# Two feature products made early, the count products moved behind x1's, and another start value for a planner's DMA clock

## The chip, the cores and the metric

One Trainium2 chip, of which one core runs the program. The metric is the time on the device in microseconds (us), the median over runs; less is better.

## The reference

A graph with 4096 nodes and 64 features, and a dense 4096 x 4096 matrix `adj` whose entries are mostly zero. Two layers, cut to what matters:

```python
# layer 0: two hops
h = relu(layernorm(x)); u = h
for k in range(2):
    u = tanh(concat([adj @ u, u], axis=1) @ W[k])     # x1, then x2
x = x + u
# layer 1
h = relu(layernorm(x)); support = h @ weight
mask = (adj != 0)
rank = cumsum(mask, axis=1); deg = rank[:, -1:]
k = minimum(deg, 100.0)
pos = rank - (deg - k)
w = mask * where(pos > 0, 0.5 ** (k - pos), 0.0)
x = x + w @ support + bias
```

## The kernel before, in words

The nodes are cut into four rows (`NCH`) of 1024 and 32 blocks (`NB`) of 128. A tile of the matrix holds one block of sources by 1024 destinations, 512 KB, and the loads of the first sweep take two blocks at once, 1 MB. Every load is issued on SyncE's queue (SP).

**Sweep 1** goes through the four rows, 16 pairs of blocks each (step `k` counts 64 pairs). For each pair TensorE (PE) adds `adj @ h` into the row's sums. A row's sums are `acc = (acc[0], acc[1])`: `acc[1]` is one PSUM bank where the two halves of 512 destinations (`c` = 0, 1) stand in partitions 0 to 63 and 64 to 127 (64-column products, L264); `acc[0]` has two banks for the blocks whose x1 is already known, where h and x1 are multiplied in one go (128-column products, L473, the "fused" blocks). Beside it VectorE (DVE) and ScalarE (ACT) mark the nonzero entries as bytes and DVE counts along them (`count_pair`), which yields codes that layer 1 turns into weights. In row 0 further work is strung between the pairs by `k`: layer norms, `features_T` (h transposed into `pre1`), and `own_share`, which multiplies a row's transposed features with the second half of W[0] and puts the product back into `pre1`.

**The end of a row** is the generator `finish_row`; sweep 1 takes one step of it per pair (`step()`), so that its parts lie between the next row's pairs. `x1_of` multiplies the sums into the bank `po`, takes in the own product, and makes tanh: rows 1 and 2 have their own product from `own_share` and DVE adds it (L221), rows 0 and 3 make it as a second product in `po` (L210). `totals` adds up the counts. `x1_and_share` makes x1 as nodes and its share of hop 2 (banks `pt`, L327), `take` copies them out on ACT. At the end `set_after` multiplies the totals with a triangle matrix (banks `pb`, L303: how many nonzeros stand in partitions behind) and makes the row's limits on DVE (L305 to L316). `settle` (L402) subtracts these limits from the codes.

**Sweep 2** starts with row 3's end (`finish_last`, the same parts in one generator, stepped after blocks 1, 3 and 5), then has two kinds of work for PE: 72 single blocks for hop 2 (`hop`, L264, each with its own load of 512 KB, L817) and 128 units of layer 1 (`layer1`, L739, 128 columns wide, each with a weight tile made by ACT, L679, or DVE, L671 and L674). When a row's hop 2 is complete, `finish_x2` makes x2, the residual, the second layer norm and the features of layer 1 (`feat`, L612 and L613).

The order of all this in sweep 2 is written out by a planner that runs when the program is built: `clock` holds a rough time for each engine and for the DMA queue, `use` advances it, and at each step the planner takes the next block if its tile should have landed (`tiles[n][3]`) or the next unit if its weights and features should be ready. The engines then run their instructions strictly in that order, whatever the real times are. Lines that matter for it:

```python
        clock["DMA"] = -7.0
...
            end = use("DMA", 1.28, t)
            tiles.append((k, r, a, end + (2.0 if t > start else LAND)))
...
            if n in (1, 3, 5):
                next(last, None)
```

Zero of these clocks is the first block of sweep 2. The last 56 units of layer 1 are kept for after the last block (`n_late`).

PSUM has two single banks, `one` and `two`, that all small products share, beside two buffers each of `acc[0]` and `acc[1]`.

Of the kernel before, what the change touches and what calls it, by code (L numbers as in the profile page):

```python
# [44 lines left out]
def gnn_kernel(  # L45
# [20 lines left out]
    nc = tc.nc  # L66
# [66 lines left out]
    def two(name="two"):  # L133
        return pone.tile([P, C], F32, tag="two", name=name)
# [68 lines left out]

    by_t = lambda ap: ap.rearrange("q (u p v) -> q u v p", u=2, v=2)

    def paired(po, terms):

        for n, (w, v) in enumerate(terms):
            for c in range(NC):
                nc.tensor.matmul(  # L210
                    po[c * D : (c + 1) * D, :], w(c), v(c),
                    start=n == 0, stop=n == len(terms) - 1,
                )

    def x1_of(po, I, terms, xs, at_=None):


        own = (lambda c: wz[:, c, 0, 1], lambda c: flat(pre1[:, chunk(I), :]))
        paired(po, terms + [own] * (at_ is None))
        if at_ is not None:  # L220
            nc.vector.tensor_tensor(at_, po, flat(pre1[:, chunk(I), :]), op=ALU.add)  # L221
            po = at_
        for c in range(NC):
            nc.scalar.activation(xs[c][:D], po[c * D : (c + 1) * D, :], AF.Tanh)

    def own_share(I):

        h = flat(pre1[:, chunk(I), :])
        po = two(name="po")
        paired(po, [(lambda c: wz[:, c, 0, 1], lambda c: h)])  # L230
        nc.scalar.copy(h, po)

    as_nodes = lambda ap: ap.rearrange("p (c t) e -> p t c e", c=NC)

# [61 lines left out]
        nc.vector.tensor_tensor(both.bitcast(U16), count(I, 0), count(I, 1), op=ALU.add)  # L296
        nc.scalar.copy(tot, both)

    def set_after(I, tot, banks):

        cols = slice(I * CW, (I + 1) * CW)
        for c, pb in enumerate(banks):
            nc.tensor.matmul(pb, tri, tot[:, c * C : (c + 1) * C], start=True, stop=True)  # L303
        for c, pb in enumerate(banks):
            nc.vector.tensor_scalar(  # L305
                after[1][:, cols][:, c * C : (c + 1) * C], pb, off, float(K), op0=ALU.add, op1=ALU.min
            )

        early = after[0][:, cols]
        nc.vector.tensor_scalar(  # L310
            early.bitcast(U16), count(I, 1), -1.0, float(FULL * 257), op0=ALU.mult, op1=ALU.add
        )
        nc.vector.tensor_tensor(
            early.bitcast(U16), early.bitcast(U16), after[1][:, cols].bitcast(U16), op=ALU.add
        )
        nc.vector.tensor_scalar(early, early, float(K), None, op0=ALU.min)  # L316
# [24 lines left out]
    def finish_row(I, acc, held):  # L341
        if I:

            T = [tmp(name="T") for _ in range(NC)]
            for c in range(NC):
                nc.scalar.copy(T[c][:D], acc[0][:D, c, :])
                nc.scalar.copy(T[c][D:], acc[1][c * D : (c + 1) * D])
            xs = [tmp(name="x1T") for _ in range(NC)]
            for c in range(NC):
                nc.scalar.copy(xs[c][D:], acc[0][D:, c, :])  # L350
            terms = [(lambda c: w0, lambda c: T[c])]
        else:
            xs = [tmp(name="x1T") for _ in range(NC)]
            S = tmp(name="S")
            nc.scalar.copy(S, acc[1])
            terms = [(lambda c: wz[:, c, 0, 0], lambda c: S)]
        both = tmp([P, CW], U8, name="both")
        yield
        x1_of(one(name="po"), I, terms, xs, T[1] if 0 < I < NCH - 1 else None)
        tot = tmp([P, CW], BF16, name="tot")  # L360
        totals(I, both, tot)
        yield
        if I:
            yield
        banks = x1_and_share(I, xs)
        take(hxs[I][:, :, D:], banks, 0)
        if I == 0:
            yield

            own = [v for k in sorted(held) for v in held[k]]  # L370
            for n, (b, a) in enumerate(own):
                agg_pair(acc[0][:, 0, :], at(b)[:, D:], a, n == 0, n == len(own) - 1)
            held.clear()
            G = tmp(name="G")
            nc.scalar.copy(G, acc[0][:, 0, :])
            yield
            g = by_t(G)
            for h, pt in halves_of(banks, 1):
                for t in range(2):
                    nc.tensor.matmul(  # L380
                        pt[:, t], g[:, h, t, :], wz[:, :, 1, 0, :],
                        start=False, stop=True, skip_group_check=True,
                    )
        take(pre1[:, chunk(I), :], banks, 1)
        yield
        set_after(I, tot, [one(name="pb"), two(name="pb")])
        all_settle(I)


# [18 lines left out]
    def sweep1():  # L408
# [28 lines left out]
        for k, (I, b) in enumerate(pairs):  # L437
            n = k % (NB // 2)
            if n == 0:
                acc = sums_of("acc")  # L440
            if k == 0:
                load(1, 0)
                load_x(2)
                load(2, 0)
                load_x(1)
                load(3, 0)
                load_x(0)
            if k == 6:
                load_weights()
            load(k + 5, k)  # L450
            if k == 0:
                next(first)
                next(first)
                rest = ln_relu(hxs[-1][:, : CB - 2, :D], pre1[:, NB - CB : b0, :])
                next(rest)
                for _ in first:
                    pass
                next(rest)
                more = ln_relu(hxs[2][:, :, :D], pre1[:, chunk(2), :])
                for _ in rest:  # L460
                    pass
                next(more)
                steps.append(more)
            if k in (2, 5):
                q = 1 - k // 3
                steps.append(ln_relu(hxs[q][:, :, :D], pre1[:, chunk(q), :]))
            a = tiles[k]
            count_pair(I, b, a, k in marked)
            for r in (1, 0):
                g = b - 1 + r  # L470
                if fused(I, g):
                    for c in range(NC):
                        nc.tensor.matmul(  # L473
                            acc[0][:, c, :], at(g), a[:, r, c * C : (c + 1) * C],
                            start=g == CB * I - 1, stop=g == 0,
                        )
                else:
                    agg_pair(acc[1], at(g)[:, :D], a[:, r], g == NB - 1, g == CB * I)
                if I == 0 and g < CB:
                    held.setdefault(k, []).append((g, a[:, r]))  # L480
            step()
            if k in (4, 6, 9, 13):
                features_T({4: 3, 6: 2, 9: 1, 13: 0}[k])
            if k in (12, 14):
                own_share({12: 2, 14: 1}[k])

            j = k + (2 if k < NB // 2 - 2 else 3)
            if j < len(tiles):
                m = j % (NB // 2)
                if m % 2 == 1 and m >= 3 if j < NB // 2 else m % 3 == 2 and m > 3:  # L490
                    mark_on_act(*pairs[j], tiles[j])
                    marked.add(j)
            if I > 1 and n % 2 == 1:
                settle()
            if n == NB // 2 - 1 and I < NCH - 1:
                steps.append(finish_row(I, acc, held))
                step()
# [12 lines left out]
    def finish_last(acc):  # L510

        I = NCH - 1
        bytes_ = mbuf.rearrange("p a r i -> p (a r i)")
        tot = bytes_[:, 2 * CW :].bitcast(BF16)
        totals(I, bytes_[:, :CW], tot)
        T, xs = ([tmp(name=n) for _ in range(NC)] for n in ("T", "x1T"))
        for c in range(NC):
            nc.scalar.copy(T[c][:D], acc[0][:D, c, :])
            nc.scalar.copy(T[c][D:], acc[1][c * D : (c + 1) * D])
        for c in range(NC):  # L520
            nc.scalar.copy(xs[c][D:], acc[0][D:, c, :])
        use("ACT", 3.4, 0.2)
        yield
        x1_of(one(name="po"), I, [(lambda c: w0, lambda c: T[c])], xs)
        use("ACT", 1.1, use("PE", 1.8) + 0.2)
        yield
        banks = x1_and_share(I, xs)
        take(hxs[I][:, :, D:], banks, 0)
        take(pre1[:, chunk(I), :], banks, 1)
        use("ACT", 1.5, use("PE", 2.0) + 0.2)  # L530
        yield
        set_after(I, tot, [one(name="pb"), two(name="pb")])
        feats[2] = place([P, CB, 2 * D], F32R, "cnt", "feat")
        use("DVE", 2.9, use("PE", 0.5) + 0.2)
        all_settle(I)
        space(feats[2].rearrange("p b d -> p (b d)"), clock["DVE"], 2)

# [262 lines left out]
    def sweep2(acc):  # L800
# [9 lines left out]
        total = len(blocks)  # L810
        accs, tiles, open_ = {}, [], {}
        n_late = 56
        clock["DMA"] = -7.0

        def load(k, r, a, t):
            I, b = blocks[len(tiles)]
# [133 lines left out]
```

## Time and profile before

| | |
|---|---|
| median of 3 runs | 349.91 us (349.72 to 350.49) |
| the profiled execution | 349.67 us |
| its span in the profile | 347.9 us |
| PE busy | 327.6 us (94%) |
| DVE, ACT busy | 266.3 us (77%), 202.9 us (58%) |
| granted TensorE clock | 0.996 |
| HBM read | 107.15 MB |
| end of row 0's loading, first block of sweep 2, last block landed | 54, 199, 308 us |

The profile is one execution of the program. An engine's busy time is the union of its instructions; "PEld" is the loading of weights into PE, beside the products. A line of the chain of waits gives a start, a duration, an engine, the tile that is written, the source line and the number of instructions. A float32 product of 512 columns shows as two matmuls. A line of the timeline ends, in brackets, with the idle time before it and what ended that. A line of the waits gives the waiting engine and line, what it waited for, the total in us, how often, and the longest.

### The profile page before, as it was taken

The page shows a single profiled execution, that of the slowest core. Times are in us where ns is not written, and L with a number is a line of the kernel's source. Part 1 is how long each engine was busy: PE and PEld are TensorE (multiplying, and loading weights), DVE is VectorE, ACT ScalarE, POOL GpSimd, SP SyncE. Part 2 cuts the span into 40 slices and gives each one's busy share as a digit, 9 for nine tenths or more (in the row PEclk, how much of TensorE's full clock was granted, in tenths as well). Part 3 has the DMA queues.
Part 4 walks back from the last instruction along what each step waited for, and adds up shares of the span by engine and source line. Part 5 has one row for each costly group of instructions (what it writes and reads, how often), then busy time and mean ns, then how long its engine had stood idle before and what let it go on. Part 6 is the DMA issues. An engine that isn't in the chain of part 4 may idle for free.

```text
span 347.9 us, 3823 instructions
## 1 busy us (share of the span) xinstructions
PE 327.6 (94%) x1360; PEld 155.6 (45%) x1360; DVE 266.3 (77%) x392; ACT 202.9 (58%) x207; POOL 23.8 (7%) x22
## 2 busy tenths in 40 slices
PE   2787899999999999999999999989999999989995
PEld 0132334333434344444444443334466645347885
DVE  4987688549959999989999927785398998269733
ACT  2097885094437634167144253256599999799940
POOL 2220200000000000000000000403000030003000
PEclk9999999999999999999999999999999999999998
DMA  7999999999999979893998899999975448930012
GB/s 255 413 409 406 411 408 410 407 410 408 409 410 409 398 303 382 304 356 121 381 338 309 298 386 367 342 417 407 409 300 183 179 145 314 401 140 0 3 43 77
DMA packets 30466, 108.44 MB, mean 312 GB/s; under 512 B 2416, under 2 KB 3824, under 8 KB 30448
## 3 DMA queue, kind: packets, MB, share of 16 engines
q1 hardware_dynamic: 30448, 108.21, 80.5%
q8 instruction: 10, 0.16, 0.2%
q14 instruction: 8, 0.07, 0.1%
HBM read 107.15 MB, written 1.05 MB: 311 GB/s over the span
## 4 chain that ended last, share of the span: by engine, by line
PE 77%; DMA 16%; DVE 2%; ACT 1%; issue 1%; POOL 1%; SPq 1%; DVEq 0%; ACTq 0%
PE acc L473 24%; PE accl L739 17%; PE acc L264 16%; PE acc_low L264 12%; DMA codes<-in_adjA_dram 11%; DMA ring<-in_adjA_dram 5%; PE pt L327 2%; PE po L210 2%; PE pto L787 2%; PE py L566 1%; POOL s L197 1%; PE pb L303 1%; ACT codes L241 1%; DVE feat L613 0%; DVE xc L200 0%
## 5 line engine op out<-in xcount | busy, mean ns | idle before, releaser
L679 ACT ACTIVATE weights<-codes 128x1024 fp32r<-128x1024 uint8 x95 | 91.6, 1044 | 14.5 <-DVE codes L402 7.8
L473 PE MATMUL acc<-ring,hx 128*128 128x512 f32 x176 | 76.4, 594 | 0.0
L264 PE MATMUL acc<-ring,hx 128*64 128x512 f32 x288 | 66.6, 599 | 0.9 <-DMA ring<-in_adjA_dram 0.9
L739 PE MATMUL accl<-weights,feat 128*128 128x512 f32 x254 | 62.4, 398 | 0.4 <-DVE feat L613 0.4
L739 PEld LDWEIGHTS accl<-weights,feat 128*128 128x128 f32 x254 | 46.3, 188 | 18.6 <-ACT weights L679 6.1
L473 PEld LDWEIGHTS acc<-ring,hx 128*128 128x128 f32 x176 | 33.4, 190 | 42.3 <-issue 42.2
L264 PE MATMUL acc_low<-codes,hx 128*64 128x512 f32 x192 | 46.1, 597 | 4.4 <-DMA codes<-in_adjA_dram 2.6
L264 PE MATMUL acc_low<-ring,hx 128*64 128x512 f32 x128 | 34.5, 657 | 9.5 <-DVE hx L200 6.2
L402 DVE TENSOR_TENSOR codes<-codes,after 128x2048 uint16<-128x2048 uint16 x32 | 38.1, 1219 | 0.1
L264 PEld LDWEIGHTS acc<-ring,hx 128*64 128x64 f32 x288 | 19.4, 136 | 39.3 <-issue 32.2
L242 ACT ACTIVATE codes<-codes 128x2048 uint8<-128x2048 int8 x19 | 36.3, 1910 | 0.6
L250 DVE TENSOR_SCALAR mbuf<-ring 128x2048 uint8<-128x2048 f32 x30 | 36.6, 1220 | 0.0
L674 DVE TENSOR_SCALAR weights<-bits 128x1024 fp32r<-128x1024 f32 x32 | 22.2, 695 | 15.0 <-PE accl L739 11.6
L241 ACT ACTIVATE codes<-ring 128x2048 int8<-128x2048 f32 x8 | 15.3, 1911 | 30.3 <-DMA ring<-in_adjA_dram 30.3
L257 DVE TENSOR_TENSOR codes<-mbuf,cnt 128x1024 uint16<-128x1024 uint16 x41 | 28.4, 692 | 1.5
L258 DVE TENSOR_SCALAR cnt<-codes 128x1024 uint16<-128x1024 uint16 x64 | 27.3, 427 | 2.2
L264 PEld LDWEIGHTS acc_low<-codes,hx 128*64 128x64 f32 x192 | 14.2, 137 | 29.7 <-issue 19.5
L241 ACT ACTIVATE codes<-codes 128x2048 int8<-128x2048 f32 x11 | 21.0, 1913 | 9.6 <-DMA codes<-in_adjA_dram 9.6
L587 POOL TENSOR_TENSOR pre<-pre,wb 128x512 f32<-128x512 f32 x4 | 5.2, 1295 | 266.3 <-DVE xc L192 266.3
L264 PEld LDWEIGHTS acc_low<-ring,hx 128*64 128x64 f32 x128 | 9.4, 147 | 29.9 <-issue 13.5
L671 DVE TENSOR_SCALAR bits<-codes 128x1024 uint32<-128x1024 uint8 x32 | 22.1, 691 | 0.7
L250 DVE TENSOR_SCALAR mbuf<-codes 128x2048 uint8<-128x2048 f32 x15 | 18.3, 1220 | 0.0
(87 smaller groups left out, 233.6 us busy)
## 6 DMA issues: line engine op xcount, KB each, us to landing
ring<-in_adjA_dram SPq DMA_DIRECT2D x74, 512.0 KB, 6.0
ring<-in_adjA_dram SPq DMA_DIRECT2D x37, 1024.0 KB, 8.2
codes<-in_adjA_dram SPq DMA_DIRECT2D x26, 1024.0 KB, 17.4
pre<-in_x_dram SPq DMA_DIRECT2D x4, 256.0 KB, 7.3
xres<-in_x_dram SPq DMA_DIRECT2D x4, 256.0 KB, 7.3
out_dram<-o SPq DMA_DIRECT2D x3, 256.0 KB, 2.6
out_dram<-o SPq DMA_DIRECT2D x2, 128.0 KB, 2.2
wb<-in_weights_dram SPq DMA_DIRECT2D x1, 192.0 KB, 17.9
```

The source lines that it names most:

```text
L241: nc.scalar.activation(sign, a, AF.Sign)
L242: nc.scalar.activation(m, sign, AF.Square, scale=float((FLAG - 1 + 0.25) ** 0.5))
L250: nc.vector.tensor_scalar(m, a, 0.0, float(FLAG - 1), op0=ALU.not_equal, op1=ALU.mult)
L257: nc.vector.tensor_tensor(q, m, cnt, op=ALU.add)
L258: nc.vector.tensor_scalar(cnt, q, 0x7F7F, None, op0=ALU.bitwise_and)
L264: nc.tensor.matmul(acc[c * D : (c + 1) * D, :], src, a[:, c * C : (c + 1) * C], start=first, stop=last,)
L402: nc.vector.tensor_tensor(q, q, a[:, None, :].to_broadcast([P, 4, CW // 2]), op=ALU.subtract)
L473: nc.tensor.matmul(acc[0][:, c, :], at(g), a[:, r, c * C : (c + 1) * C], start=g == CB * I - 1, stop=g == 0,)
L671: nc.vector.tensor_scalar(state["bits"], q, float(ZERO), ONE, op0=ALU.subtract, op1=ALU.mult)
L674: nc.vector.tensor_scalar(w, state["bits"].bitcast(F32), 2.0 ** (127 - LOW), None, op0=ALU.mult)
L679: nc.scalar.activation(w, q, AF.Exp, scale=LN2, bias=BIAS)
L739: nc.tensor.matmul(sums[g][:, c, :], feats[J][:, k, :], w[:, c * C : (c + 1) * C], start=first, stop=last,)
```

## The change

Own products: `own_share` is now also called for row 3 (step 10) and for row 0 (step 15). Row 3's product goes back into `pre1`, as those of rows 1 and 2 do, and its x1 takes DVE's addition. Row 0's stays in the bank `one` as an unfinished sum; the product with the row's sums is added in the same bank later. Count products: the two matmuls of `set_after` become `count_after`, which stands directly behind `x1_and_share`, and write into the banks of the row's sums, which have been read by then, instead of `one` and `two`. DVE's part stays where it was. The planner's costs for these parts follow, and its clock for the DMA queue starts at −10.5 instead of −7.0.

```diff
-    def paired(po, terms):
+    def paired(po, terms, first=True, last=True):
...
-                    start=n == 0, stop=n == len(terms) - 1,
+                    start=first and n == 0, stop=last and n == len(terms) - 1,
...
     def x1_of(po, I, terms, xs, at_=None):
-        own = (lambda c: wz[:, c, 0, 1], lambda c: flat(pre1[:, chunk(I), :]))
-        paired(po, terms + [own] * (at_ is None))
+        paired(po, terms, at_ is not None)
...
+    own0 = []
+
     def own_share(I):
         h = flat(pre1[:, chunk(I), :])
-        po = two(name="po")
-        paired(po, [(lambda c: wz[:, c, 0, 1], lambda c: h)])
-        nc.scalar.copy(h, po)
+        po = two(name="po") if I else one(name="po")
+        paired(po, [(lambda c: wz[:, c, 0, 1], lambda c: h)], last=I > 0)
+        if I:
+            nc.scalar.copy(h, po)
+        else:
+            own0.append(po)
...
-    def set_after(I, tot, banks):
-
-        cols = slice(I * CW, (I + 1) * CW)
+    def count_after(I, tot, acc):
+
+        banks = [acc[0][:, c, :] for c in range(NC)] if I else [acc[1], acc[0][:, 1, :]]
         for c, pb in enumerate(banks):
             nc.tensor.matmul(pb, tri, tot[:, c * C : (c + 1) * C], start=True, stop=True)
+        return banks
+
+    def set_after(I, banks):
+
+        cols = slice(I * CW, (I + 1) * CW)
...
     # finish_row
-        x1_of(one(name="po"), I, terms, xs, T[1] if 0 < I < NCH - 1 else None)
+        x1_of(one(name="po") if I else own0.pop(), I, terms, xs, T[1] if I else None)
...
         banks = x1_and_share(I, xs)
+        counts = count_after(I, tot, acc)
...
-        set_after(I, tot, [one(name="pb"), two(name="pb")])
+        set_after(I, counts)
...
     # sweep1
-            if k in (12, 14):
-                own_share({12: 2, 14: 1}[k])
+            if k in (10, 12, 14, 15):
+                own_share({10: 3, 12: 2, 14: 1, 15: 0}[k])
...
     # finish_last
-        x1_of(one(name="po"), I, [(lambda c: w0, lambda c: T[c])], xs)
-        use("ACT", 1.1, use("PE", 1.8) + 0.2)
+        x1_of(one(name="po"), I, [(lambda c: w0, lambda c: T[c])], xs, T[1])
+        use("ACT", 1.1, use("DVE", 0.7, use("PE", 0.9) + 0.2) + 0.1)
         yield
         banks = x1_and_share(I, xs)
+        counts = count_after(I, tot, acc)
...
-        use("ACT", 1.5, use("PE", 2.0) + 0.2)
+        use("ACT", 1.5, use("PE", 2.4) + 0.2)
         yield
-        set_after(I, tot, [one(name="pb"), two(name="pb")])
+        set_after(I, counts)
         feats[2] = place([P, CB, 2 * D], F32R, "cnt", "feat")
-        use("DVE", 2.9, use("PE", 0.5) + 0.2)
+        use("DVE", 2.9, clock["PE"])
...
     # sweep2
-        clock["DMA"] = -7.0
+        clock["DMA"] = -10.5
```

## The prediction, made before the changed kernel was run

> **What bounds the kernel now.** I read the page's busy times first, then the waits of TensorE from the end of row 0's loading on, then the chain of waits, and last the timeline around the places that the change touches.
>
> ```profile
> PE 327.6 (94%) x1360; PEld 155.6 (45%) x1360; DVE 266.3 (77%) x392; ACT 202.9 (58%) x207; POOL 23.8 (7%) x22
> ```
>
> ```profile
> PE accl L739 <- DVE feat L613: 1.6, 2, 1.1
> PE acc L264 <- DMA ring<-in_adjA_dram: 0.9, 2, 0.8
> PE po L210 <- ACT S L355: 0.3, 1, 0.3
> ```
>
> The three lines are all that TensorE (PE) waited for from 54 to 345 us: 2.8 us. From row 0's finish on the kernel is a queue of PE work, and whatever leaves that queue shortens it. Before 54 us it is otherwise: PE was busy 40.2 of 54.4 us there (windows), waiting for tiles of the matrix that land about every 2.6 us. Work put there, before the last tile of row 0, can be free. The chain of waits prices what the change moves:
>
> ```profile
> 54.40 1.94 PE po L210 x8
> 56.34 1.72 PE acc_low L264 x8
> ...
> 102.23 1.23 PE po L210 x3
> ...
> 109.40 1.87 PE acc_low L264 x8
> 111.27 0.54 PE pb L303 x2
> 111.80 7.02 PE acc_low L264 x32
> ...
> 201.00 2.09 PE po L210 x7
> ```
>
> Row 0 makes two products into po (1.94); row 1 makes one (1.23, and 0.37 behind one interleaved matmul: 1.60 together); row 3 makes two (2.09 and 0.38, 2.47). A pair of blocks takes 1.72 behind other 64-column work but 1.87 behind 128-column work such as pt or pb; the eight-matmul groups in 7.02 are 4 x 1.72 and again 0.14 more. So a change of width into the narrow products costs 0.15. The two count matmuls stand between narrow pairs in every row and pay it.
>
> ```profile
> 41.26 1.91 ACT L242 ACTIVATE codes<-codes 128x2048 uint8<-128x2048 int8 x1
> ...
> 43.73 1.06 PE L210 MATMUL po<-pre,wz 128*64 128x512 f32 x4
> ...
> 44.44 1.91 ACT L241 ACTIVATE codes<-codes 128x2048 int8<-128x2048 f32 x1 [1.27 <-DMA codes<-in_adjA_dram]
> ...
> 53.29 0.57 ACT L231 COPY pre<-po 128x512 f32<-128x512 f32 x1
> ...
> 227.76 0.73 PE L739 MATMUL accl<-feat 128*128 128x512 f32 x2 [1.15 <-DVE feat L613]
> ```
>
> ACT has a hole of 1.27 us before 44.44, set by a landing. PE stands idle 1.15 us at the start of layer 1, waiting for features.
>
> **The change part by part.** The sum is made against the profiled execution: 349.67 us, a span of 347.9 and 1.8 around it. It is 0.24 under the median of the three runs, 349.91. 0.2% is 0.7 us, about what can be told from no change (the runs lie 0.8 apart).
>
> *Row 0's own product.* Its four matmuls (1.06 us busy, 0.86 of the queue's pitch: half a pair's 1.72) go from behind S to the end of row 0's last pair, about 51.5 us. There PE waits for the next tile until 52.11, and then for S until 54.40 (0.35). S itself is set by ACT (own copy of row 1 at 53.29 to 53.86, then S), which nothing here lengthens. The pair at 52.1 starts perhaps 0.3 later and still ends before 54.4. Gain 0.86; if S came earlier, the cover would be 0.3 thinner. Bank and operand are ready: features of row 0 are copied at 48.67 to 49.32.
>
> *Row 3's own product into row 0.* It is issued behind the tenth pair, near 38.5 us; the next pair waits for its landing at 39.34, so 0.1 at most is pushed. Its ACT copy (0.57, as L231) queues behind the mark that ends at 43.17 and ends at 43.74, inside the 1.27 hole; behind it on ACT is the mark at 44.44, which waits for its data anyway. Row 2's own product needs the same bank: it ran at 43.73, so it moves 0.1. Row 1's own product waited 0.6 for the copy before it (PEld po, ACT pre), which takes that up. Cost 0; without that cover, 0.57.
>
> In row 3's finish 0.87 of PE goes (2.47 to 1.60). In its place DVE adds (0.69) before tanh. Row 2, which does this already, shows po at 148.18, add at 150.05, tanh at 150.78 to 152.06: 3.88 us from po to x1. Put at row 3's po, 200.83, x1 is ready at 204.71, against 204.76 now; but the two blocks between now end at 204.3. PE would wait 0.45 before pt. Net gain 0.4. Queued behind the add on DVE are about five subtractions of L402 (1.22 each), then the row's limits: 203.4 + 6.1 = 209.5, and they start at 209.54 now. Nobody is delayed, and nobody gains.
>
> *Counts behind pt.* Both are 128 columns wide, so two width changes per row go: 0.15 into the narrow pairs and about 0.11 into pb (0.54 against two 512-column passes of 0.215). 0.25 a row, 1.0 for four rows; in row 0 the 0.65 of pb may give 0.1 more, left out. The bounds are 0 (if pt's drain is only moved) and 0.4. The operand tot is there: cast at 57.48 to 58.51 in row 0, at 105.95 to 106.99 in row 1, while pt ends at 60.1 and 109.4. The new banks were last read by copies that x1 needed. DVE idles 7.7 and 6.95 us for pb now (L305); in row 0 it would run ahead, but PE, and not DVE, sets that stretch.
>
> *New clock.* No work changes; the order of PE's queue does. Up to tile 41 the planner counts tiles as 1.28 us apart from its start value, so from −7.0 tile 23 is expected at 27.6 and tile 33 at 41.0 us after the first block, from −10.5 at 24.1 and 37.5. The trace has the first block at 199.06 and tile 23 landing at 225.12 (26.1), tile 24 at 226.37 (27.3), tile 33 at 239.87 (40.8). With row 3's 0.87 off, the loads that wait for its blocks come that much earlier: 25.2, 26.4, 39.9. So the old clock is late by up to 2.4 and the new one early by 1.1 to 2.4. What it wins: tile 24 is planned ahead of layer 1's start, so one block (0.86) fills the 1.15 hole; I take 0.5 of it, bounds 0 and 1.15. What it costs: a block queued before its tile stalls PE. The traced blocks in 28 to 49 us start 0.40 to 1.99 after landing at the ends of their bursts; shifted by 3.5 − 0.87 and a lag of PE behind the plan of 0.3 to 1.0, they would be up to 1.5 too early. Tiles land 1.28 apart, so a stall is paid once and not for each tile. I take 0.7, bounds 0 and 2.4.
>
> For tile 31 fifteen of the sixteen landing updates are in at 235.97 and the last at 237.31; it stays 1.3 behind to tile 49. One late DMA engine thus makes the 2.4.
>
> **Sum.** 0.86 + 0.4 + 1.0 + 0.5 − 0.7 = 2.1. 349.67 − 2.1 = 347.6; from the median 347.8. I say 347.6.
>
> **Rivals.** *Late tiles take about half of it.* Stall 1.5 to 2.4 instead of 0.7: 348.4 to 349.3. For it: one lagging engine, as traced. Against it: the lag is not the clock's doing and may fall elsewhere.
>
> *Slower by the new order.* The blocks moved forward outrun their tiles in the first half (2.4), and the last ten blocks do too: there the traced blocks start 0.04 to 0.6 after landing, waits 0.9 in all, the loads being released by blocks twelve and more before them. If the new order sends that release 2 us later against the blocks, each late tile is waited for: 2.4 + 2.0 against gains of 2.8, so 1.6 slower, 351.3. It decides once stalls together exceed 3.5. The last tile is followed by a fixed 56 units of layer 1, so nothing wins it back. Against it: the loads at the end are released by consumption, not by the rough clock.
>
> *Slower tiles.* If the pitch that the planner sees were not 1.28 but 1.39, as (260.92 − 210.83)/36 from tile 13 to 49 with all interruptions, and the lag of 1.3 came on top again, tile 33 would be another 20 x 0.11 = 2.2 late: stall 2.9, time 349.8. Against it: between the interruptions the landings keep 1.28, 410 GB/s. The Trainium skill, DMA: Bandwidth & Descriptors, Specifications, gives a core some 358 GB/s of HBM, an estimated 1.46 us for such a tile of 512 KB, by which the stall would be near 4 and the time 351; here the trace disagrees with it.
>
> *Nothing arrives at the end.* The last of the 72 tiles lands at 308.41 and PE waits for it. If the loads there are what counts and not PE, 349.2 to 350.6. Against it: each load there waits for a block of PE, so it moves with PE.
>
> *The parts don't act.* Pt's drain stays and x1 of row 3 is no sooner: 0.86 and 0.5 − 0.7, 349.0. Against it: row 2's own figures.
>
> **Numbers.** Forecast (346.4 to 348.3) 0.46; half taken 0.18; nothing arrives 0.10; slower tiles 0.02; parts don't act 0.06; slower 0.18. Faster by over 0.2%: 0.46 + 0.16 + 0.05 = 0.67; within: 0.02 + 0.10 + 0.02 + 0.01 = 0.15; slower 0.18. The range leaves out the far slower cases and the largest gain (all bounds at their best: 0.86 + 0.87 + 1.4 + 1.15, 4.3): 346.2 to 350.8.
>
> **What would show it.** Po in row 0 one product of about 1.1 at 54.4 and the next pair at 55.3; po in row 3 about 1.6 and then a short wait for x1T before pt; pb with no narrow pair ahead of it and some 0.43 long; sweep 2's first block at 197.3 to 197.7 instead of 199.06; the idle time before the first accl under 0.7; waits of acc for ring tiles between 28 and 49 us after the first block. Wrong would be: the first block no earlier than 198.4, or ring waits over 3 in all.

## The result, and the profile after

| | before | changed |
|---|---|---|
| median of 22 runs | 349.93 us (348.71 to 351.4) | 348.13 us (347.33 to 350.21) |
| ratio, 95% interval | | 0.9949 (0.9935 to 0.9964) |
| the profiled execution, its span | 349.67, 347.9 | 349.98, 347.3 |

The change is 1.8 us faster (1.3 to 2.3). The profiled execution of the changed kernel is the second longest of its 22, so its span (0.6 less) understates that by about 1 us; a second profile is among the runs below. On the page:

```profile
PE 328.1 (94%) x1356; PEld 154.7 (45%) x1360; DVE 274.0 (79%) x402; ACT 199.9 (58%) x204; POOL 24.6 (7%) x22
```

TensorE's (PE's) waits from 54 to 345 us (total, times, longest):

```profile
PE accl L750 <- DVE feat L624: 1.0, 1, 1.0
PE acc L268 <- DMA ring<-in_adjA_dram: 0.7, 3, 0.3
PE py L577 <- DVE S L568: 0.5, 1, 0.5
PE po L210 <- ACT S L364: 0.2, 1, 0.2
PE accl L750 <- DVE weights L685: 0.2, 1, 0.2
```

PE waits 2.6 us in all, as before (2.8), but in other places: the 1.15 ahead of the first accl is gone, and the 1.0 is now the wait for row 0's features near the end. The chain of waits (start, duration, in us) at the places that the change touches:

```profile
54.32 1.08 PE po L210 x4
55.40 1.72 PE acc_low L268 x8
57.12 2.08 PE pt L336 x16
59.20 0.32 PE acc_low L307
59.52 0.15 issue
59.67 1.94 PE acc_low L268 x8
...
101.01 1.23 PE po L210 x3
...
154.27 0.15 issue
154.41 1.94 PE acc_low L268 x8
156.35 41.40 PE acc L483 x96
197.75 1.87 PE acc L268 x8
199.62 1.23 PE po L210 x3
...
202.99 2.30 PE pt L336 x16
```

For row 2 the chain of the kernel before reads:

```profile
153.45 2.08 PE pt L327 x16
155.53 1.87 PE acc_low L264 x8
157.40 0.54 PE pb L303 x2
157.93 41.20 PE acc L473 x96
199.13 1.87 PE acc L264 x8
```

Row 0 makes one product (1.08) where it made two (1.94). The count products (L307, now written into the sums' banks) stand behind pt, 0.47 with the step behind them; one of their two records is missing from the trace in most rows, and the "issue" is its place. Row 1's first product into po starts 1.22 earlier than before, the first block of sweep 2 1.38; 0.08 of both is the earlier start of row 0's end (54.32 against 54.40).

### The profile page after: what moved, and what is told of

The parts are those of the page before. It is cut to its first block, busy times and chain, and to the rows that moved or that the text cites. A ratio compares the mean times of both kernels' runs of the same rounds, so it can differ in the third digit from the quotient of the medians.

```text
span 347.3 us, 3829 instructions
## 1 busy us (share of the span) xinstructions
PE 328.1 (94%) x1356; PEld 154.7 (45%) x1360; DVE 274.0 (79%) x402; ACT 199.9 (58%) x204; POOL 24.6 (7%) x22
## 3 DMA queue, kind: packets, MB, share of 16 engines
HBM read 107.15 MB, written 1.05 MB: 312 GB/s over the span
## 4 chain that ended last, share of the span: by engine, by line
PE 73%; DMA 18%; ACT 3%; issue 2%; DVE 2%; SPq 1%; ACTq 0%; DVEq 0%
PE acc L483 24%; PE acc L268 17%; PE accl L750 12%; PE acc_low L268 12%; DMA codes<-in_adjA_dram 11%; DMA ring<-in_adjA_dram 7%; PE pt L336 2%; PE pto L798 2%; ACT weights L690 2%; PE po L210 2%; PE py L577 1%; DVE weights L685 1%; ACT codes L245 1%; DVE bits L682 0%; PE pt L390 0%
## 5 line engine op out<-in xcount | busy, mean ns | idle before, releaser
L690 ACT ACTIVATE weights<-codes 128x1024 fp32r<-128x1024 uint8 x90 | 86.7, 1044 | 12.7 <-PE accl L750 9.8
L750 PE MATMUL accl<-weights,feat 128*128 128x512 f32 x254 | 63.5, 400 | 1.3 <-DVE feat L624 1.0
L685 DVE TENSOR_SCALAR weights<-bits 128x1024 fp32r<-128x1024 f32 x37 | 26.6, 719 | 7.1 <-PE accl L750 3.7
L682 DVE TENSOR_SCALAR bits<-codes 128x1024 uint32<-128x1024 uint8 x37 | 25.6, 691 | 0.8
L261 DVE TENSOR_TENSOR codes<-codes,cnt 128x1024 uint16<-128x1024 uint16 x19 | 13.1, 690 | 8.4 <-ACT codes L246 7.6
```

What stands on the lines that cost most here:

```text
L261: nc.vector.tensor_tensor(q, m, cnt, op=ALU.add)
L682: nc.vector.tensor_scalar(state["bits"], q, float(ZERO), ONE, op0=ALU.subtract, op1=ALU.mult)
L685: nc.vector.tensor_scalar(w, state["bits"].bitcast(F32), 2.0 ** (127 - LOW), None, op0=ALU.mult)
L690: nc.scalar.activation(w, q, AF.Exp, scale=LN2, bias=BIAS)
L750: nc.tensor.matmul(sums[g][:, c, :], feats[J][:, k, :], w[:, c * C : (c + 1) * C], start=first, stop=last,)
```

## The experiments

Row 0's S product is the first product of row 0's end: its sums, copied to S, go into po. What lies ahead of it, in which PE waits for tiles, is not the same in every execution: it starts at 53.28 to 54.82 in the fourteen profiles of eleven kernels, with no visible link to what was changed, and 0.04, 0.47 and 0.57 apart in the three kernels that have two profiles. So stretches behind that point are compared, all in us. Up to block 14 of sweep 2 they repeat within 0.02 us in every kernel that has the same work there.

| kernel | row 0's S product to first block of sweep 2 | first block to block 6 | S product to block 14 | block 14 to PE's end | timed median |
|---|---|---|---|---|---|
| before (two profiles) | 144.66, 144.66 | 10.59, 10.59 | 163.41, 163.41 | 126.55, 127.39 | 349.93, 350.4 |
| changed (two) | 143.36, 143.36 | 9.74, 9.74 | 161.20, 161.21 | 128.26, 128.01 | 348.13, 348.15 |
| clock_only | 144.67 | 10.58 | 163.41 | 127.60 | 350.21 |
| old_clock (two) | 143.36, 143.36 | 9.74, 9.73 | 161.20, 161.19 | 127.26, 127.35 | 348.78, 348.53 |
| own_only | 143.80 | 9.95 | 161.90 | 127.30 | 349.3 |
| counts_only | 144.20 | 10.39 | 162.70 | 126.55 | 348.9 |
| counts_late | 143.68 | 9.94 | 161.78 | 127.53 | 348.53 |
| hold_dve | 143.36 | 9.74 | 161.21 | 126.91 | 347.78 |
| late64 | 143.36 | 9.74 | 161.20 | 127.04 | 347.74 |
| hold64 | 143.36 | 9.73 | 161.20 | 127.36 | 348.14 |
| old64 | 143.34 | 9.74 | 161.19 | 127.96 | 348.97 |

### One part at a time

**clock_only**

```diff
 # before
-        clock["DMA"] = -7.0
+        clock["DMA"] = -10.5
```

> Only the planner's DMA clock goes from -7.0 to -10.5; all work as before. Theory A (the gain is PE work taken off the queue, each part by itself): the 1.15 us hole before layer 1 is filled by a block, and up to 1.5 us of waits for tiles come in, so between 1.0 faster and 1.0 slower than before; first block of sweep 2 at 199.1 as before. Rival B (the new order of sweep 2 is what makes the change faster): 1.5 us or more faster than before.

Ratio to before 1.0006 (0.9989 to 1.0024): no difference. PE's wait for features fell from 1.6 to 0.9 us (the hole ahead of layer 1 is gone, row 0's at the end has grown), its waits for tiles stayed at 0.9. Rival B falls.

**old_clock**

```diff
 # changed
-        clock["DMA"] = -10.5
+        clock["DMA"] = -7.0
```

> The whole change but for the clock, which stays at -7.0. Theory A: first block of sweep 2 at 197.7, hole before layer 1 about 1.1 again, 1.5 to 2.3 us faster than before. Rival B: within 0.7 us of before.

Ratio 0.9954 (0.9935 to 0.9974), the change's own gain within the intervals. But the hole ahead of layer 1 did not stay at 1.1:

```profile
224.74 0.74 PE L750 MATMUL accl<-feat 128*128 128x512 f32 x2 [1.94 <-DVE feat L624]
```

This line of the timeline shows the first unit of layer 1 with the idle time before it in brackets. Ahead of it stand nine blocks from block 14 on (36 matmuls, four to a block), where the kernel before has ten (40). With about 1 us less planned PE work, the old clock has tile 23 land behind the features, and block 23 moves behind the first units. The real features did not come sooner against block 14 (9.89 us behind its start, 9.95 before), so the hole grew by one block. The new clock closes it: in the changed kernel 26 blocks and one more py lie ahead of the first unit, and none of its waits is for those features.

**own_only**

```diff
 # changed, clock at -7.0
-        counts = count_after(I, tot, acc)      # in both places
...
-        set_after(I, counts)
+        set_after(I, count_after(I, tot, [one(name="pb"), two(name="pb")]))
```

> Only the own products of rows 0 and 3 are moved (with the planner's costs for row 3's product); count products stay where they were, in the two single banks, and the clock at -7.0. Theory A: 0.86 in row 0 and 0.65 in row 3, no change in rows 1 and 2: first block of sweep 2 at 198.2, in all 1.0 to 1.6 us faster than before. Rival B: within 0.7 us of before.

Ratio 0.9975 (0.9955 to 0.9996). Row 0: 0.86 up to the first block, to the hundredth as expected. Row 3: 10.59 to 9.95, 0.64. In all 1.51 up to block 14; behind it 0.3 is lost against the two profiles of before (127.30 against 126.97), where the same grown hole (1.95) stands. The time alone would not have decided: the gain is 0.9 by the ratio (0.1 to 1.6) and 0.6 by the medians, 349.3 against 349.86 beside it, less than was expected.

**counts_only**

```diff
 # before
         banks = x1_and_share(I, xs)
+        counts = count_after(I, tot, acc)
...
-        set_after(I, tot, [one(name="pb"), two(name="pb")])
+        set_after(I, counts)
```

> Only the count products are moved behind x1's, into the banks of the finished sums (with the planner's costs for that); own products and the clock as before. Theory A: two changes of width less in rows 0, 1 and 3 and one in row 2, 0.28 + 0.25 + 0.11 + 0.25 = 0.9 us less PE time; first block of sweep 2 at 198.5; in all 0.5 to 1.0 us faster. Rival C (the width costs nothing by itself; what row 0 gained was the wait for the shared banks): only row 0 gains, 0.3, first block at 198.8.

Ratio 0.997 (0.9954 to 0.9986). Row by row, from one row's first product into po to the next row's: row 0 −0.29, row 1 −0.26, row 2 +0.09, row 3 (first block to block 6) −0.20, and −0.05 from block 6 to block 14, in all 0.71. Theory A but for row 2, where it had 0.11; rows 1 and 3 gain too, so it is not rival C alone.

**counts_late**, to tell the place from the banks:

```diff
 # changed
-        counts = count_after(I, tot, acc)      # in both places
...
-        set_after(I, counts)
+        set_after(I, count_after(I, tot, acc))
```

> The changed kernel with the count products back at their old place, between narrow pairs, but still in the banks of the finished sums. Theory A (width): from row 0's S product to the first block of sweep 2 0.45 longer than in the change (143.8 against 143.36 us), row 3's part 0.2 longer; 0.3 to 0.8 slower than the change. Rival C (banks): row 0 as in the change, nothing lost, 143.36.

0.32 is lost up to the first block, between the 0.45 of theory A and the nothing of rival C, and 0.20 more in row 3; own_only, which differs from this kernel in the banks (and the clock), is 0.12 longer than it up to the first block, all in row 0. Up to block 14 it is 161.78 against the change's 161.20 and own_only's 161.90: of 0.70 the place makes 0.58 and the banks 0.12, so rival C explains a sixth. In its chain of waits, rows 1 and 2 read

```profile
107.76 1.87 PE acc_low L268 x8
109.62 0.54 PE acc L307 x2
110.16 7.02 PE acc_low L268 x32
...
153.89 1.87 PE acc_low L268 x8
155.76 0.54 PE acc L307 x2
156.29 41.20 PE acc L482 x96
```

In row 1 narrow pairs follow the counts and pay 0.14 (7.02 against 4 x 1.72). In row 2 the 128-column fused products follow. The order there is pt, pair, counts, fused products before, and pt, counts, pair, fused products in the change: two changes of width in both, so there was none to save. The pair's own entry stays, and the fused products, now directly behind the narrow pair, take 41.40 in place of 41.20.

The Trainium skill, TensorEngine Tiling (Array Packing), Key Properties, says that a change of tiling mode, and not a change of tile alone, drains the engine. The trace agrees, with 0.15 us for an entry into the 64-column products; the page gives no figure.

### What sweep 2 gives back

Behind block 14 the changed kernel is longer than before, 128.1 against 127.0 as means of two profiles. Second profiles:

> The changed kernel once more, for a second profile. Theory D (in sweep 2 the new order loses again what it wins, at fixed places): waits for tiles of 0.2 to 0.7 us in all between 26 and 40 us after the first block, a wait of py for S of about 0.5 and a hole before row 0's units of about 1.0, as in the first profile; time 1.3 to 2.2 us under before. Rival E (the first profile was a disturbed execution): these waits gone, 144.5 us or less from the first block to PE's end, against 146.1 there.

The waits came again: 0.4 for tiles, 0.46 for S, 0.94 for row 0's features, 145.86 us from the first block to PE's end. So the waits for S and features belong to the order, and rival E falls for them. The waits for tiles do not: hold_dve and late64 below have the same order of PE's work up to their last ten blocks or further, and waited 0 and 0.3 for tiles. The median was 348.15 again (0.995, 0.9937 to 0.9964).

> The kernel before once more, for a second profile. If the stretch from row 0's S product to PE's end is a property of the kernel, it is 290.0 us again within 0.3, whatever the start (54.4 in the first profile) is, and the changed kernel wins 0.5 to 0.8 there by its two profiles, so that the other 1.0 of the median's gain must come from before row 0's S. If that stretch varies, it is 291 here.

290.8 and not 290.0 from row 0's S product to PE's end; the median is 350.4, ratio 1.0004 (0.9988 to 1.002). The difference is in the end of the loads:

```profile
PE accl L739 <- DVE feat L613: 1.3, 2, 0.9
PE acc L264 <- DMA ring<-in_adjA_dram: 1.2, 3, 0.8
PE po L210 <- ACT S L355: 0.3, 1, 0.3
```

The last block started 0.8 later against block 14 (91.44 against 90.64), with waits for tiles at 299.7, 301.0 and 308.0. The stretch of the kernel before varies there; the changed kernel has the last tile 1.38 us ahead of its block (0.04 before), so this wait is gone from both its profiles. The two pairs of profiles differ by 1.05 us from S product to PE's end, the medians by 1.8.

**hold_dve.** After the last block DVE copies its sums (S) to start the chain that ends in row 0's features. In the changed kernel's timeline:

```profile
306.18 0.69 DVE L682 TENSOR_SCALAR bits<-codes 128x1024 uint32<-128x1024 uint8 x1
...
306.97 0.69 DVE L685 TENSOR_SCALAR weights<-bits 128x1024 fp32r<-128x1024 f32 x1
307.58 0.68 DVE L568 COPY S<-acc 128x512 f32<-128x512 f32 x1
...
308.32 1.21 PE L577 MATMUL py<-wz,S 128*128 128x128 f32 x8 [0.47 <-DVE S L568]
...
320.94 8.00 PE L750 MATMUL accl<-weights,feat 128*128 128x512 f32 x32 [0.97 <-DVE feat L624]
```

The last block ended at 306.27; DVE was at a weight tile, and S came 1.3 later. Everything behind it on DVE, ACT and GpSimd is one chain, so the features came later too. In the order of old_clock it is ACT that makes this copy, 0.05 behind the block's end, and py does not wait.

```diff
 # changed
-                state["dve"] and late and dve + 1.4 <= d_end and dve <= clock["PE"] + 3.0
+                state["dve"] and not state["hold"] and late and dve + 1.4 <= d_end and dve <= clock["PE"] + 3.0
...
+            state["hold"] = total - 3 <= n < total
```

> The changed kernel, but VectorE makes no weights before the last three blocks' end, so that it is free to copy the last block's sums. Theory D: S starts within 0.2 us of the last block's end instead of 1.3 behind, the wait of py (0.5) goes and the hole before row 0's units shrinks from 1.0 to 0.5 or less; 0.5 to 1.0 faster than the change. Rival F (ScalarE's weights, not the chain of features, set the end): the hole shrinks, but the units behind it wait for weights as much longer; within 0.3 of the change.

```profile
305.78 0.69 DVE L568 COPY S<-acc 128x512 f32<-128x512 f32 x1 [0.19 <-PE acc L268]
...
319.15 2.06 PE L750 MATMUL accl<-weights,feat 128*128 128x512 f32 x8 [0.43 <-DVE feat L624]
```

S is right behind the last block, py does not wait, the hole is 0.43, and block 14 to PE's end is 1.1 to 1.35 shorter than in the changed kernel. Most of that is not the edit's. Up to the last block PE's order is the same in both kernels, and this execution, which waited for no tile, went from block 14 to block 60 in 73.32, against 74.38 and 74.14 in the changed kernel's two. From block 60 to PE's end the changed kernel takes 53.88 and 53.86, counts_late, with the same order, 53.86, and hold_dve 53.60: by the profiles the edit is worth 0.27. The waits that it takes away are larger, but PE then waits for ACT's weights:

```profile
PE accl L750 <- ACT weights L690: 0.4, 2, 0.2
PE accl L750 <- DVE feat L624: 0.4, 1, 0.4
```

That is rival F in the main, and less than the 0.5 to 1.0 of theory D. The median is 347.78, ratio to before 0.994 (0.9926 to 0.9955); it is 0.37 under the changed kernel beside it, 348.15, and the intervals overlap.

**late64**

```diff
 # changed
-        n_late = 56
+        n_late = 64
```

> The changed kernel with 64 instead of 56 units of layer 1 kept for after the last block. Theory D: 24 more or so units lie over the chain of features, the hole before row 0's units (1.0) is closed, 0.3 to 1.0 faster than the change. Rival F: units that are kept wait for weights at the end, no faster or slower by up to 1.

The hole is closed (no wait of accl for features), waits for weights of ACT are 0.4, block 14 to PE's end 127.04. From block 60 on it takes 53.33, 0.54 less than the changed kernel; the rest of the shorter stretch is again fewer waits for tiles ahead of that. Median 347.74, ratio 0.9941 (0.992 to 0.9961): as much as hold_dve, and by the same hole; here too the intervals overlap with the changed kernel's.

**hold64** has both edits.

> The changed kernel with VectorE held free before the last three blocks and 64 units kept for after the last block. If both close the same hole, no better than either alone: 347.5 to 348.0. If each takes its own wait away (S late; too few units), 347.0 to 347.5.

Median 348.14, a little above both expectations, ratio 0.9936 (0.9913 to 0.9959), 127.36 in the profile and 53.60 from block 60 on: no better than either. Both close one hole; what is left there are four waits of accl for ACT's weights, 0.8 in all.

**old_again, old64**

> The change with the clock at -7.0 once more. If the order that the new clock makes is worth nothing, its median is within 0.7 us of the changed kernel's 348.15, and its stretch from row 0's S product to PE's end 288.5 again. If the new clock is a loss, as the profiles say (288.5 against 289.2 and 289.5), it is 0.5 or more below 348.15.

Median 348.53, ratio 0.9966 (0.9946 to 0.9986), stretch 288.54 again. By the profiles the old clock's order is 0.7 to 1.0 shorter than the new one's; the medians say 0.4 and 0.65 longer, within the intervals. hold_dve's execution gained about as much (0.8 to 1.1) ahead of its edit, in the new order itself, by not waiting for tiles. So what the new clock is worth beside the rest isn't settled; no comparison puts it above 1 us.

> The change with the clock at -7.0 and 64 units kept for after the last block. Theory D: the hole of 0.8 before row 0's units is closed as in the other order, 287.7 from row 0's S product to PE's end and a median 0.5 to 0.8 under that of the same kernel with 56. Rival F: nothing.

Median 348.97, ratio 0.9977 (0.9958 to 0.9996), 289.15: it gained nothing. The expected 287.7 and 0.5 to 0.8 failed. The hole of 0.8 before row 0's units went, but the stretch grew by 0.6; waits for ACT's weights (0.6) and a tile (0.2) came in, and the rest is not accounted for. What 64 is worth depends on the order it meets.

## Why the prediction was right

It forecast 347.6 us (346.2 to 350.8) and 2.1 us off the profiled execution; measured are 348.13 and 1.8. The mechanism is shown for the parts that take work off PE. That the total fits as well as it does is in part luck: two terms were mis-sized by 0.24 and 0.29 in opposite directions, the loss behind the last block was not in the sum, and 0.75 of the gain in the medians is not in the profiles' stretches.

- **A queue of PE work, each part by itself**: shown. Own products 1.51 and counts 0.71 make 2.22 up to block 14; the change has 2.21.
- **Row 0's own product, 0.86**: measured 0.86. In the changed kernel it runs at 51.40, as forecast, and the next pair at 52.25. That row 0's S product would start no later is not shown more closely than the 0.6 by which two executions of one kernel differ there.
- **Row 3's product in row 0, cost 0**: its copy runs on ACT at 42.98 instead of the 43.17 that was worked out, and ACT's mark still waits 0.80 for its tile at 44.35. Row 2's product ran at 43.64. No cost.
- **Row 3's finish, net 0.4**: mis-sized; 0.64 to 0.65. The wait for x1 was put at 0.45 ahead of pt. The add came 1.86 behind the first product as in row 2 (201.31), and x1 was whole at 203.32, 3.87 behind it, as worked out (3.88). But pt's first two matmuls need only the first half of x1, ready at 202.67; they ran at 202.92, the third, which waits for the second half, at 203.37. So pt started without waiting and took 2.30 instead of 2.08: 0.22 of waiting, inside it.
- **Counts, 1.0**: mis-sized; 0.71. The step that failed is that the counts "stand between narrow pairs in every row", 0.25 a row: in row 2 wide products follow and nothing is saved (+0.09). Rows 0, 1 and 3 gave 0.29, 0.26 and 0.20. In row 0 the 0.1 that was left out is the banks' 0.12.
- **Clock, 0.5 − 0.7**: the sum near zero fits (1.0006 alone; old and new clock not told apart). Both pieces are real: the hole of 1.15 is filled, and tiles are waited for, 0.7 and 0.4 in the two profiles, where 0.7 was taken. Blocks 24 and 30 to 34 start 0.04 to 0.43 behind their tiles in the first, so a little lag more or less decides: hold_dve, in the same order, waited for none. Missed was that without the new clock the hole would grow to 1.94.
- **"A fixed 56 units" behind the last block**: wrong for the changed kernel. 58 units follow, and the chain of features starts 1.3 late. From the last block to PE's end it takes 38.5 us, 35.9 before; two units of some 0.47 are 0.9 of that, the wait for S (0.47), the longer wait for features (0.97 against 0.42) and one for ACT's weights (0.15) another 1.2, and about 0.5 is not accounted for. This is what took a part of the gain. How much of it the late S costs is less than its waits say: with S in time, hold_dve won 0.27, because PE then waits for ACT's weights.
- **Slower by the new order** did not come; its place, the last ten tiles, became the opposite: the new order has them 1.4 to 20 us early, and it is the kernel before that waits there (0.9 and 1.2). Of its last ten blocks six started 0.04 to 0.6 behind their tiles, as the prediction says, the other four 1.0 to 2.3.

Open is 0.75 of the 1.8: the profiles, two of each, show 1.05 from the S product on. The start up to it differed by up to 0.57 between two executions of one kernel, the way from block 14 to block 60, with its waits for tiles, by up to 1.06 in one order of PE's work; neither was seen in the timed runs, so the cause of this part stays open.

## What to carry to other kernels

Where one engine's queue sets the time, price a moved instruction at the place it leaves and at the place it enters, its neighbours included: here the two count products of a row cost 0.15 to 0.26 more between narrow products than behind wide ones, and nothing more where wide ones followed. A planner that writes out a fixed order turns saved work into a different order; look for the hole that grows by one whole step, and at the end, where a latency chain hangs on one small copy, look whether the engine that makes the copy is free, and then for the wait that takes over: here it left 0.27 of the gain. Two profiles of one order differed by 1 us here on the way through the tiles that are waited for, so compare a stretch behind the last of these waits.

## What the runs showed of the hardware

The last of a tile's sixteen landing updates can fall 1.2 to 1.5 us behind the other fifteen and stay there for some twenty tiles. In the first profile of before it is so from tile 31 (fifteenth update 235.97, last 237.31) to tile 49; in the changed kernel from tile 30 (232.79 and 234.20) to tile 54. The pitch of 1.28 us stays, and the block waits for the last update. The Trainium skill, DMA: Bandwidth & Descriptors, says in its section on why a DMA increments its semaphore by 16 that the engines of one transfer finish independently and that only the full count means landed; the trace agrees, and gives the size.

The lag is not the same in every execution, and where blocks follow closely on their tiles it shows as waits: at tile 31 it was 1.40 in the changed kernel's first profile, 1.27 in its second, 1.25 in hold64, 0.6 in hold_dve and 0.5 in late64. In the same sequence these five executions, whose order of PE's work is the same there, took 27.34, 27.09, 26.80, 26.29 and 26.67 us from block 14 to block 36; the last of them had waited 0.27 for tile 24, ahead of that lag.

The start of the program, in which PE waits for loads, moved by 0.04 to 0.57 us between two executions of one kernel and by 1.5 over all fourteen profiles, while the PE work behind it, 144 us to the first block of sweep 2, repeated to 0.02.
